# Four residual graph layers on one core: a division of the last projection put under program order, and the denominators of the second half placed at later tiles

## The chip, the core and the metric

The kernel runs on one core of a Trainium2 chip. The core's engines are TensorE (PE, with its weight loads), VectorE (DVE), ScalarE (ACT), GpSimd (POOL) and SyncE (SP, which here only issues DMAs). The metric is the device time of one launch in microseconds. Times of several launches are given by their median; one launch was also taken by the hardware profiler, and all lines of the trace come from that one.

## The reference

A graph of N = 3327 nodes with 512 features a node goes through four layers. Each computes `x = layernorm(x + layer(x, adj))`, row by row.

```
def _L2_gnn_ref(h, adj, W, a):
    ...
    Wh = (h @ W).reshape(n, H, D)
    a1, a2 = (a[0, :, :D], a[0, :, D:])
    s1 = jnp.einsum('nhd,hd->nh', Wh, a1)
    s2 = jnp.einsum('nhd,hd->nh', Wh, a2)
    e = jax.nn.leaky_relu(s1[:, None, :] + s2[None, :, :], negative_slope=ALPHA)
    att_logits = jnp.where(adj[:, :, None] > 0, e, NEG_BIG)
    attention = jax.nn.softmax(att_logits, axis=1)
    h_prime = jnp.einsum('ijh,jhd->ihd', attention, Wh)
    return jax.nn.elu(h_prime.reshape(n, H * D))
...
    x = _layernorm(x + _L0_gnn_ref(x, adj, L0_gnn_W, L0_gnn_a), axis=-1)
    x = _layernorm(x + _L1_gnn_ref(x, adj, L1_gnn_W_nb, L1_gnn_b_nb, L1_gnn_W_line, L1_gnn_b_line, 64), axis=-1)
    x = _layernorm(x + _L2_gnn_ref(x, adj, L2_gnn_W, L2_gnn_a), axis=-1)
    x = _layernorm(x + _L3_gnn_ref(x, adj, L3_gnn_W, L3_gnn_a), axis=-1)
    return x
```

Layers 0, 2 and 3 are such attentions (8 heads of 64, 8 of 64, 4 of 128; layer 0 has no elu). Layer 1 takes the mean over the first 64 neighbours of each node and adds two linear maps with a leaky relu.

The kernel leaves the division by the softmax's sum until after `att @ h`: it collects the unnormalised rows (`hd` in HBM) and the sums, and divides when the rows are read for the next layer. elu is computed as `max(h, 0) + min(exp(h), 1)`, whose constant of one falls out in the layernorm that follows.

## The kernel before

**Tiles.** The rows are cut into NT = 26 tiles of 128, counted from 0, so "the fifth tile" is tile 4. The first 13 (tiles 0 to 12) and the last 13 (tiles 13 to 25) are the two halves; the attention works on one half's output rows at a time.

**Stages in time.** Projection of layer 0 (to about 143 us), attention 0 (to 960), the `sage` stage of layer 1 (linear maps to about 1155, then the sums over neighbours to 1620), attention 2 (from about 1640 to 2552), the last projection in `third` (2552 to 2690), attention 3 and the last norms (to the end). Between two layers a "finish" turns the attention's raw rows into the next layer's input.

**The finish (`finish_steps`, L165 to L203, and `norm_rows`, L146 to L161)** takes a pair of tiles, t0 and t0+1. Its steps are:
- `load`: `h` of both tiles from `hd` (L126, on SP in the last projection), and the residual input `xr` from POOL.
- `divide(s)`: on DVE, `h` times the reciprocal of the sums `rec` (L181). With elu, ACT's `e = exp(h)` follows (L186). If `pinned` is set, `exp` of s = 0 is kept in program order.
- `add(s)`: on DVE, L194 and L195 with elu, L197 without.
- `norm_rows` for both tiles together: statistics of each on DVE (L152, L153), one square root on ACT for the pair (L154), reciprocal and product on DVE (L155, L158), then scale and shift of each tile on ACT (L161). As the square root and the two small DVE steps are shared, neither tile of a pair is ready before both have been divided and added.

Exp and square root are in different tables of ACT; a change between them shows as ACT_TABLE_LOAD.

**The last projection (`third`, L892 to L942).** Its loop goes over pairs t0 = 0, 2, ..., 24. Groups of finish steps are loaded ahead by `load_group` (L911): pairs 2 and 4 before the loop, pair t0+6 in iteration t0. Each tile is stored (L133, SP), transposed on PE (`project1`, L261), copied out of PSUM by ACT (`xT`, L262) and summed by DVE (`xsum`, L263). After the first tile of a pair, the finish of the next waiting pair is put in. Then the tile before is multiplied by the weights (`project2`, L271: sixteen matmuls), ACT takes three small columns (L272, L275), and DVE makes `vt` in two pieces (L277), which SP stores (L283). After tile 14 `prepare` and `cut` (L299 to L352) set up the first half of the attention, with transposes of its columns on PE (L312) and their copies by ACT (L314). `mean` (L286) ends the stage. In `load_group`, `pinned` is set for the pair t0 = 2 alone.

**The second half's sums.** Attention 0 and 2 leave two steps in `late` (L541): `place`, 16 small DMAs that bring the sums of tiles 13 to 25 into SBUF (L517, on SP), and `finish_sums` (L525 to L538), five DVE instructions that make their reciprocals. `sage` (L757) and `third` (L923) take these two steps out of the list at t0 = 4 and t0 = 8. Tile 13, the first that needs them, is the second of the pair t0 = 12.

**What orders the work.** PE's instructions run in program order. Those of the other engines are put in order by a scheduler when the program is built, by its own estimates of when each is ready; `tc.keep_in_program_order(ins)` takes an instruction out of its hands, so that it stays behind what the program wrote before it on that engine.

Of the kernel before, what the change touches and what calls it, by code (L numbers as in the profile page):

```python
# [32 lines left out]
def kernel(  # L33
# [10 lines left out]
    nc = tc.nc  # L44
# [74 lines left out]
    def load_tile(dst, src, t, eng):  # L119

        if src.shape[0] == N and t == NT - 1 and LAST < P:
            nc.gpsimd.memset(dst, 0.0)
            for a, z in _row_pieces(LAST):
                eng.dma_start(out=dst[a:z, :], in_=src[t * P + a:t * P + z, :])
        else:
            eng.dma_start(out=dst, in_=src[t * P:(t + 1) * P, :])  # L126
# [38 lines left out]
    def finish_steps(pool, xin, layer, t0, n, hbufs=6, eng=nc.sync, xbufs=None, xpool=None, ebufs=None, pinned=False):  # L165
        H, D = layer.H, layer.D
        ys, xs, steps = [], [], []

        def load():
            for t in range(t0, t0 + n):  # L170
                h = pool.tile([P, F], F32, name="h", bufs=hbufs)
                load_tile(h, hd, t, eng)
                ys.append(h)
                xr = xpool.tile([P, F], F32, name="xr", tag="hb") if xpool else \
                    pool.tile([P, F], F32, name="xr", bufs=xbufs)
                load_tile(xr, xin, t, nc.gpsimd)
                xs.append(xr)

        def divide(s):
            h = ys[s]  # L180
            nc.vector.tensor_tensor(h.rearrange("p (h d) -> p h d", h=H), h.rearrange("p (h d) -> p h d", h=H),  # L181
                                    rec[:, t0 + s, :H].rearrange("p (h e) -> p h e", e=1).to_broadcast([P, H, D]),
                                    op=ALU.mult)
            if layer.elu:
                e = pool.tile([P, F], F32, name="e", bufs=ebufs)
                ins = nc.scalar.activation(e, h, AF.Exp)  # L186
                if pinned and s == 0:
                    tc.keep_in_program_order(ins)
                xs.append(e)

        def add(s):
            h, xr = ys[s], xs[s]
            if layer.elu:
                nc.vector.scalar_tensor_tensor(xr, xs[n + s], 1.0, xr, op0=ALU.min, op1=ALU.add)  # L194
                nc.vector.scalar_tensor_tensor(h, h, 0.0, xr, op0=ALU.max, op1=ALU.add)  # L195
            else:
                nc.vector.tensor_tensor(h, h, xr, op=ALU.add)  # L197

        steps.append(load)
        for s in range(n):  # L200
            steps += [lambda s=s: divide(s), lambda s=s: add(s)]
        steps.append(lambda: norm_rows(pool, ys, t0))
        return ys, steps  # L203
# [482 lines left out]
    def sage(first, first_pool, xin, prev, nxt, wsrc, dst):  # L686
# [3 lines left out]
        with tc.tile_pool(name="sg_z", bufs=1, reuse_waits="tile") as zp, \  # L690
# [21 lines left out]
            with tc.tile_pool(name="sa_w", bufs=1, reuse_waits="tile") as wp, \  # L712
                    tc.tile_pool(name="sa", bufs=2, reuse_waits="tile") as fp, \
                    tc.tile_pool(name="sa_t", bufs=2, reuse_waits="tile") as sp, \
                    tc.tile_pool(name="sa_ps", bufs=2, space=PSUM, reuse_waits="tile") as ps:
                wn = load_w(wp, wnT, "wn", nc.gpsimd)
                wl = load_w(wp, wlT, "wl", nc.gpsimd)
                blb = wp.tile([P, F], F32, name="blb")
                nc.gpsimd.dma_start(out=blb, in_=bl.to_broadcast([P, F]))

                def step1(xt):
                    pt = ps.tile([P, FC, P], F32, name="pt")
                    for c in range(FC):
                        nc.tensor.transpose(pt[:, c, :], xt[:, c * P:(c + 1) * P], ident)  # L724
                    xT = sp.tile([P, FC, P], F32, name="xT")
                    nc.scalar.copy(xT, pt)  # L726
                    return xT

                def step2(xt, xT, t):
                    pz = ps.tile([P, F], F32, name="pz")  # L730
                    for c in range(FC):
                        nc.tensor.matmul(pz, xT[:, c, :], wn[:, c, :], start=c == 0, stop=c == FC - 1)  # L732
                    pi = ps.tile([P, F], F32, name="pi")
                    for c in range(FC):
                        nc.tensor.matmul(pi, xT[:, c, :], wl[:, c, :], start=c == 0, stop=c == FC - 1)  # L735
                    nc.scalar.copy(zs(t, 0), pz)
                    r1 = sp.tile([P, F], F32, name="r1")
                    nc.vector.tensor_tensor(r1, pz, zs(t, 0), op=ALU.subtract)
                    nc.scalar.copy(zs(t, 1), r1)
                    z3 = sp.tile([P, F], BF, name="z3")  # L740
                    nc.vector.tensor_tensor(z3, r1, zs(t, 1), op=ALU.subtract)
                    nc.sync.dma_start(out=zd[t * P:(t + 1) * P, :], in_=z3)
                    xi = sp.tile([P, F], F32, name="xi")
                    nc.vector.tensor_tensor(xi, pi, blb, op=ALU.add)
                    nc.vector.scalar_tensor_tensor(xi, xi, 0.01, xi, op0=ALU.mult, op1=ALU.max)
                    nc.vector.tensor_tensor(xi, xi, xt, op=ALU.add)
                    nc.sync.dma_start(out=xid[t * P:(t + 1) * P, :], in_=xi)


                cr = fp.tile([NT, P], BF, name="cr", bufs=1)  # L750
                nc.sync.dma_start(out=cr, in_=ctd[NT:NT + 1, :].rearrange("o (t p) -> (o t) p", p=P))
                cnt = zp.tile([P, 3, NT], F32, name="cnt")
                pend = None
                ahead = first
                for t0 in range(0, NT, 2):
                    ys = ahead
                    if t0 in (4, 8):  # L757
                        prev.late.pop(0)(fp)
                    if t0 == 8:
                        cf = fp.tile([NT, P], F32, name="cf", bufs=1)  # L760
                        nc.scalar.copy(cf, cr)
                        pt = ps.tile([P, FC, P], F32, name="pt")
                        cb = pt[:, 0, :NT]
                        nc.tensor.transpose(cb, cf, ident[:NT, :NT])
                        nc.vector.tensor_scalar(cnt[:, 0, :], cb, NEIGHBOURS, 1.0, op0=ALU.min, op1=ALU.max)
                        nc.vector.reciprocal(cnt[:, 1, :], cnt[:, 0, :])
                        nc.vector.tensor_scalar(cnt[:, 2, :], cb, 0.0, None, op0=ALU.is_gt)
                    for s, y in enumerate(ys):
                        xT = step1(y)
                        if s == 0 and t0 + 2 < NT:  # L770
                            ahead = finish(fp, xin, prev, t0 + 2, 2, 6, nc.sync if t0 else nc.gpsimd)
                        if pend:
                            step2(*pend)
                        pend = (y, xT, t0 + s)
                step2(*pend)
            first_pool.close()

            with tc.tile_pool(name="sb_w", bufs=1, reuse_waits="tile") as wp, \
# [69 lines left out]
                for b in range(len(blocks)):  # L848
                    t0, i0 = blocks[b]
# [42 lines left out]
    def third(first):  # L892
        with tc.tile_pool(name="col3", bufs=1) as cp, tc.tile_pool(name="at_r3", bufs=2, reuse_waits="tile") as rp:
# [3 lines left out]
            with tc.tile_pool(name="p_w", bufs=1, reuse_waits="tile") as wp, \  # L897
# [13 lines left out]
                def load_group(t0):  # L911
                    if t0 < NT:
                        groups.append(finish_steps(fp, x2, L2, t0, 2, 10, nc.gpsimd if t0 < 4 else nc.sync, 6,
                                                    pinned=t0 == 2))
                        groups[-1][1].pop(0)()

                load_group(2)
# [2 lines left out]
                load_group(4)  # L920
                for t0 in range(0, NT, 2):
                    ys = ahead
                    if t0 in (4, 8):  # L923
                        L2.late.pop(0)(fp)
                    load_group(t0 + 6)
                    for s, y in enumerate(ys):
                        t = t0 + s
                        store_tile(x3, y, t, nc.sync)
                        xT = L3.project1(pp, ps, y, t)
                        if s == 0 and groups:  # L930
                            ahead, steps = groups.pop(0)
                            for f in steps:
                                f()
                        if pend:
                            L3.project2(pp, bank, wsb, *pend)
                        pend = (xT, t)
                        if t == HALF + 1:
                            L3.prepare(pp, 0)
                            L3.first_rows = L3.rows(rp, 0, 0)
                            L3.cut(pp, 0)  # L940
# [284 lines left out]
```

## Time and profile before

| | us |
|---|---|
| median of 3 launches | 3389.97 |
| lowest, highest | 3388.6, 3393.65 |
| the profiled launch's own time | 3389.15 |
| its span in the trace | 3387.4 |
| PE, DVE, ACT busy in the span | 3251.2, 2687.5, 2354.6 |
| last projection, 2552 to 2690: PE, DVE, ACT busy in 138 us | 119.66, 111.95, 100.71 |
| linear maps of `sage`, 960 to 1155: PE, DVE, ACT busy in 195 us | 179.47, 129.87, 66.36 |

The profile is read like this. The page gives the busy time of each engine and its costliest groups; the waits list says which engine stood idle ahead of which line, and what it waited for; the timeline lists instructions in order of time with the start, the time taken, the engine, the line and the tiles written and read, and in brackets the idle time just before. Several equal instructions in a row are merged into one row with their count. The mean clock that PE was granted over the whole launch was 0.985 of full speed; in the last projection 0.91, in the linear maps of `sage` 0.96.

### The profile page before, as it was taken

The numbers are of one execution on the slowest core, as the hardware profiler recorded it, in microseconds if no ns is written. First come the engines' busy times: TensorE is split into PE (matmuls) and PEld (weight loads), VectorE is DVE, ScalarE is ACT, GpSimd is POOL, SyncE is SP. The second block draws the span as 40 slices with busy tenths as digits, with TensorE's granted clock in tenths as the row PEclk, the third lists the DMA queues.
The fourth block names the chain that finished last, engine by engine and source line by source line (L and its number), as shares of the span: only waits on it lengthen the run. The fifth ranks groups of instructions, "written<-read, shape, count | busy, mean of one in ns | idle before, by whom it ended". The sixth has DMA issues, their size and how long they took to land.

```text
span 3387.4 us, 47182 instructions
## 1 busy us (share of the span) xinstructions
PE 3251.2 (96%) x18476; PEld 1626.4 (48%) x18476; DVE 2687.5 (79%) x2619; ACT 2354.6 (70%) x2143; POOL 239.8 (7%) x389
## 2 busy tenths in 40 slices
PE   8899999999979999999989999999998999999997
PEld 7634344444434445545544444444446754455453
DVE  5799999999967544444449999999998766668887
ACT  2398998999953333333338999999997655558986
POOL 3100000000010011111110000000002000010110
PEclk9999999999999999999999999999998999999998
DMA  9644111110143343333320111111117411122211
GB/s 368 222 124 127 49 49 38 55 49 28 44 123 125 122 117 84 91 85 87 80 77 20 47 48 50 51 48 47 35 31 241 152 41 42 41 51 80 94 42 49
DMA packets 288014, 284.29 MB, mean 84 GB/s; under 512 B 107492, under 2 KB 223534, under 8 KB 287791
## 3 DMA queue, kind: packets, MB, share of 16 engines
q1 hardware_dynamic: 254063, 170.62, 16.6%
q0 software_dynamic: 28208, 102.96, 9.5%
q10 hardware_dynamic: 5520, 7.69, 0.7%
q8 instruction: 146, 2.39, 0.3%
q14 instruction: 77, 0.63, 0.1%
HBM read 212.01 MB, written 69.17 MB: 83 GB/s over the span
## 4 chain that ended last, share of the span: by engine, by line
PE 85%; DVE 5%; DMA 4%; ACT 3%; issue 2%; SPq 0%; ACTq 0%; DVEq 0%; POOL 0%; POOLq 0%
PE po L428 52%; PE acc L859 12%; PE pd L380 7%; PE pw L271 5%; DVE t L405 3%; PE pz L732 3%; DMA raw<-in_adjT_dram 3%; PE pi L735 3%; ACT y L408 1%; PE pt L456 1%; PE pk L819 1%; DMA h<-hd 0%; PE pa L1108 0%; PE pt L724 0%; PE pct L664 0%
## 5 line engine op out<-in xcount | busy, mean ns | idle before, releaser
L405 DVE SCALAR_TENSOR_TENSOR t<-rb,qc,mask 128x1664 f32<-128x1664 f32 x1040 | 1960.3, 1954 | 169.4 <-PE po L428 147.3
L408 ACT ACTIVATE y<-t,bi,sc 128x1664 fp8e4<-128x1664 f32 x1040 | 1769.5, 1766 | 310.4 <-PE pd L380 292.7
L428 PE MATMUL po<-t,vj 128*64 128x448 f32 (+3 forms) x8320 | 1909.6, 521 | 22.1 <-DVE t L405 19.6
L428 PEld LDWEIGHTS po<-t,vj 128*64 128x64 f32 (+1 forms) x8320 | 838.9, 148 | 970.6 <-issue 704.0
L859 PE MATMUL acc<-zs,kt 128*128 128x512 bf16 x1352 | 401.1, 380 | 0.0
L271 PE MATMUL pw<-wsb,xT 128*128 128x264 f32 (+1 forms) x1248 | 302.2, 397 | 15.2 <-DVE vt L277 12.0
L859 PEld LDWEIGHTS <-kt 128*128 128x128 fp8e4 x2002 | 196.1, 98 | 242.1 <-issue 7.7
L811 ACT CAST pk<-cy 128x512 f32<-128x512 bf16 x169 | 99.0, 588 | 277.4 <-DVE kt L823 266.3
L271 PEld LDWEIGHTS pw<-wsb,xT 128*128 128x128 f32 x1248 | 241.1, 197 | 60.7 <-ACT xT L262 10.8
L380 PE MATMUL pd<-y,sden 128*32 128x448 fp8e4 (+1 forms) x4160 | 259.5, 342 | 10.4 <-ACT y L408 10.4
L859 PE MATMUL acc<-zl,kt 128*128 128x512 bf16 x650 | 246.5, 379 | 0.0
L380 PEld LDWEIGHTS <-sden 128*32 128x32 bf16 x4160 | 117.5, 96 | 162.5 <-issue 139.8
L823 DVE SCALAR_TENSOR_TENSOR kt<-pk,mask 128x512 fp8e4<-128x512 f32 x169 | 116.1, 688 | 94.0 <-PE pk L819 94.0
L277 DVE TENSOR_TENSOR vt<-pw,dc 128x256 f32<-128x256 f32 x156 | 59.0, 418 | 148.2 <-ACT dc L272 143.7
L359 POOL DMA_DIRECT2D rb<-r x40 | 21.3, 532 | 1670.4 <-DVE t L405 1652.2
L275 ACT COPY rc<-pw 128x8 f32<-128x8 f32 (+1 forms) x78 | 12.6, 162 | 156.6 <-PE pw L271 154.1
L831 DVE SCALAR_TENSOR_TENSOR y<-acc,cnt,bnb 128x512 f32<-128x512 f32 x26 | 19.5, 751 | 97.7 <-PE acc L859 90.3
L732 PE MATMUL pz<-wn,xT 128*128 128x512 f32 x208 | 94.9, 600 | 1.7 <-ACT xT L726 1.7
L700 POOL DMA_DIRECT2D cy<-ctd x91 | 67.9, 746 | 385.1 <-ACT pk L811 312.6
L735 PE MATMUL pi<-wl,xT 128*128 128x512 f32 x208 | 93.5, 592 | 0.0
L634 DVE TENSOR_SCALAR mask<-raw 128x832 fp8e4<-128x832 int32 (+2 forms) x90 | 54.8, 614 | 38.9 <-DMA raw<-in_adjT_dram 38.5
L154 ACT ACT_TABLE_LOAD x45 | 57.7, 1283 | 37.0 <-DVE mv L153 36.4
(187 smaller groups left out, 1699.3 us busy)
## 6 DMA issues: line engine op xcount, KB each, us to landing
vj<-v SPq DMA_DIRECT2D x312, 128.0 KB
rb<-r POOLq DMA_DIRECT2D x40, 832.0 KB, 4.8
raw<-in_adjT_dram SPq DMA_DIRECT2D x67, 416.0 KB
cy<-ctd POOLq DMA_DIRECT2D x78, 256.0 KB, 4.0
h<-hd SPq DMA_DIRECT2D x61, 256.0 KB
v<-vt SPq DMA_DIRECT2D x50, 256.0 KB
hd<-hb SPq DMA_DIRECT2D x48, 256.0 KB
xr<-x POOLq DMA_DIRECT2D x45, 256.0 KB, 3.1
```

The source lines that it names most:

```text
L271: nc.tensor.matmul(pw[e][:, :FW + H], xT[:, c, :], wsb[:, c, e, :], start=c == 0, stop=c == FC - 1)
L277: nc.vector.tensor_tensor(vt[:, hs, :], pw[e][:, :FW].rearrange("p (h d) -> p h d", d=D), self.dc[:, t, hs].rearrange("p (h e) -> p h e", e=1)
L380: nc.tensor.matmul(pd[c][32 * kk:32 * kk + 32, :w_], lhsT, rhs, start=(kk, c) not in seen, skip_group_check=final is not None, stop=last a ...
L405: nc.vector.scalar_tensor_tensor(t, rb[k], self.qc[:, j, h:h + 1], mask[:, j, i0:i0 + IW], op0=ALU.max, op1=ALU.mult)
L408: nc.scalar.activation(y, t, AF.Sigmoid, bias=self.bi[:, j, h:h + 1], scale=self.sc[:, j, h:h + 1], saturate=False)
L428: nc.tensor.matmul(po[c][k * D:(k + 1) * D, :z - a_], vj[:, j % 2, k * D:(k + 1) * D], ts[k][:, a_:z], start=j == 0, stop=j == NT - 1)
L700: nc.gpsimd.dma_start(out=cy[:, :n, :], in_=ctd[t:t + n, b * GW:(b + 1) * GW] .rearrange("(o t) i -> o t i", o=1).to_broadcast([P, n, GW]))
L732: nc.tensor.matmul(pz, xT[:, c, :], wn[:, c, :], start=c == 0, stop=c == FC - 1)
L735: nc.tensor.matmul(pi, xT[:, c, :], wl[:, c, :], start=c == 0, stop=c == FC - 1)
L811: nc.scalar.copy(pks[k % 2], carry[b, t // 4 * 4][:, t % 4:t % 4 + 2, :])
L823: nc.vector.scalar_tensor_tensor(kt, pk, NEIGHBOURS, mask[:, t:t + 2, i0:i0 + GW], op0=ALU.is_le, op1=ALU.mult, saturate=False)
L859: nc.tensor.matmul(acc, kts[t][:, s * P:(s + 1) * P], zs(t, c) if c < 2 else zl[:, t, :], start=t == 0 and c == 0, stop=t == NT - 1 and c ...
```

## The change

Two things are changed.
- In `finish_steps`, the division of a pair's first tile is kept in program order whenever `pinned` is true, and the exp only when it is 2. In `load_group`, the pair t0 = 2 gets 2 (division and exp pinned), the pair t0 = 4 gets True (division alone), and all others False. The program puts the finish of the pair 4 behind the norm of the pair 2 and behind `xsum` of tile 2.
- The two `late` steps are taken at t0 = 6 and t0 = 10, both in `sage` and in `third`.

```
--- before.py
+++ after.py
@@ -178,13 +178,15 @@
 
         def divide(s):
             h = ys[s]
-            nc.vector.tensor_tensor(h.rearrange("p (h d) -> p h d", h=H), h.rearrange("p (h d) -> p h d", h=H),
+            ins = nc.vector.tensor_tensor(h.rearrange("p (h d) -> p h d", h=H), h.rearrange("p (h d) -> p h d", h=H),
                                     rec[:, t0 + s, :H].rearrange("p (h e) -> p h e", e=1).to_broadcast([P, H, D]),
                                     op=ALU.mult)
+            if pinned and s == 0:
+                tc.keep_in_program_order(ins)
             if layer.elu:
                 e = pool.tile([P, F], F32, name="e", bufs=ebufs)
                 ins = nc.scalar.activation(e, h, AF.Exp)
-                if pinned and s == 0:
+                if pinned == 2 and s == 0:
                     tc.keep_in_program_order(ins)
                 xs.append(e)
 
@@ -754,7 +756,7 @@
                 ahead = first
                 for t0 in range(0, NT, 2):
                     ys = ahead
-                    if t0 in (4, 8):
+                    if t0 in (6, 10):
                         prev.late.pop(0)(fp)
                     if t0 == 8:
                         cf = fp.tile([NT, P], F32, name="cf", bufs=1)
@@ -911,7 +913,7 @@
                 def load_group(t0):
                     if t0 < NT:
                         groups.append(finish_steps(fp, x2, L2, t0, 2, 10, nc.gpsimd if t0 < 4 else nc.sync, 6,
-                                                    pinned=t0 == 2))
+                                                    pinned=(t0 == 2) * 2 or t0 == 4))
                         groups[-1][1].pop(0)()
 
                 load_group(2)
@@ -920,7 +922,7 @@
                 load_group(4)
                 for t0 in range(0, NT, 2):
                     ys = ahead
-                    if t0 in (4, 8):
+                    if t0 in (6, 10):
                         L2.late.pop(0)(fp)
                     load_group(t0 + 6)
                     for s, y in enumerate(ys):
```

More of the change, by code (lines that the diff above doesn't have):

```diff
@@ L180, in divide @@
             h = ys[s]
-            nc.vector.tensor_tensor(h.rearrange("p (h d) -> p h d", h=H), h.rearrange("p (h d) -> p h d", h=H),
+            ins = nc.vector.tensor_tensor(h.rearrange("p (h d) -> p h d", h=H), h.rearrange("p (h d) -> p h d", h=H),
                                     rec[:, t0 + s, :H].rearrange("p (h e) -> p h e", e=1).to_broadcast([P, H, D]),
                                     op=ALU.mult)
+            if pinned and s == 0:
+                tc.keep_in_program_order(ins)
             if layer.elu:
@@ L186, in divide @@
                 ins = nc.scalar.activation(e, h, AF.Exp)
-                if pinned and s == 0:
+                if pinned == 2 and s == 0:
                     tc.keep_in_program_order(ins)
@@ L756, in sage @@
                     ys = ahead
-                    if t0 in (4, 8):
+                    if t0 in (6, 10):
                         prev.late.pop(0)(fp)
@@ L913, in load_group @@
                         groups.append(finish_steps(fp, x2, L2, t0, 2, 10, nc.gpsimd if t0 < 4 else nc.sync, 6,
-                                                    pinned=t0 == 2))
+                                                    pinned=(t0 == 2) * 2 or t0 == 4))
                         groups[-1][1].pop(0)()
@@ L922, in third @@
                     ys = ahead
-                    if t0 in (4, 8):
+                    if t0 in (6, 10):
                         L2.late.pop(0)(fp)
```

## The prediction

> **What bounds the kernel now.** I read the page first (TensorE busy in 96% of the span, and no table of slices shows a hole), then the waits of the last projection, 2552 to 2690 us, then each engine's instructions there in order of time. The projection computes one tile of 128 rows at a time on PE: four transposes (L261), sixteen matmuls of the tile before (L271). [...] First the waits of that window (total us, times, longest):
>
> ```profile
> DVE h L181 <- DMA h<-hd: 6.1, 3, 4.5
> ...
> PE pt L261 <- ACT h L161: 11.8, 2, 8.5
> ```
>
> PE waits for normalised rows, and DVE once for a load. PE in order of time (start, us, in brackets the idle time before):
>
> ```profile
> 2573.51 1.12 PE L261 MATMUL pt<-ident,h 128*128 128x128 f32 x4 [8.46 <-ACT h L161]
> 2574.42 5.42 PE L271 MATMUL pw<-wsb,xT 128*128 128x260 f32 x16
> 2579.68 0.60 PE L261 MATMUL pt<-ident,h 128*128 128x128 f32 x4
> 2580.12 3.67 PE L271 MATMUL pw<-wsb,xT 128*128 128x260 f32 x16
> 2583.63 0.60 PE L261 MATMUL pt<-ident,h 128*128 128x128 f32 x4
> ...
> 2601.26 3.77 PE L271 MATMUL pw<-wsb,xT 128*128 128x260 f32 x16 [0.98 <-ACT xT L262]
> ...
> 2616.71 0.60 PE L261 MATMUL pt<-ident,h 128*128 128x128 f32 x4
> 2618.61 3.75 PE L271 MATMUL pw<-wsb,xT 128*128 128x260 f32 x16 [1.30 <-ACT xT L262]
> ...
> 2634.75 0.75 PE L312 MATMUL pr<-ident,rc 128*4 128x128 f32 x5 [3.64 <-ACT rr L314]
> 2635.34 0.60 PE L261 MATMUL pt<-ident,h 128*128 128x128 f32 x4
> 2635.77 5.36 PE L271 MATMUL pw<-wsb,xT 128*128 128x260 f32 x16
> ```
>
> Tiles 2, 4 and 12 start their transposes at 2573.51, 2583.63 and 2616.71. From transpose to transpose a tile takes 3.95 us (2583.63 less 2579.68); the one after the long wait 6.17. After tile 15 every row follows without a wait, so the stage ends as late as PE's waits make it. Now DVE and ACT:
>
> ```profile
> 2562.96 1.40 DVE L181 TENSOR_TENSOR h<-h,rec 128x512 f32<-128x512 f32 x2 [4.52 <-DMA h<-hd]
> 2564.28 0.69 DVE L194 SCALAR_TENSOR_TENSOR xr<-e,xr 128x512 f32<-128x512 f32 x1
> ...
> 2602.73 0.20 DVE L532 SCALAR_TENSOR_TENSOR rec<-pes,rec 128x52 f32<-128x52 f32 x1
> ```
> ```profile
> 2572.65 1.52 ACT L161 ACTIVATE h<-h,rs 128x512 f32<-128x512 f32 x2
> ...
> 2578.36 1.52 ACT L161 ACTIVATE h<-h,rs 128x512 f32<-128x512 f32 x2 [0.16 <-DVE rs L158]
> ...
> 2615.69 1.52 ACT L161 ACTIVATE h<-h,rs 128x512 f32<-128x512 f32 x2 [0.79 <-DVE rs L158]
> ```
>
> DVE stood 4.52 us on tile 4's division with the additions of tiles 2 and 3 behind it. The three ACT rows end the norms of the pairs (2,3), (4,5), (12,13). The first of two is done after some 0.81 us: tile 4 at 2579.17, 4.5 us before PE takes it; tile 12 at 2616.50, 0.2 us before. One has room, the other none.
>
> [...] sixteen matmuls take 3.67 us, but 5.42 after 8.46 idle and 5.36 after 3.64; 3.75 after 1.30. [...] The trace has 1.28 us[...]. I use 1.28.
>
> **The change part by part.** From the instruction order of both built programs: PE's is identical, POOL swaps one pair. In the last projection DVE, ACT and SP change; in the sage stage the denominators move.
>
> *Tile 2.* The pinned division of tile 4 leaves its place, but the unpinned divisions of tiles 5, 6 and 7 move up into it, ahead of the additions of 2 and 3. Tile 4's load is in at 2562.96; 256 KB follow each other at some 400 GB/s (the page of 2550 to 2572 us shows 385 to 411 there), so 0.65 us apart: estimate 2563.6, 2564.3, 2564.9 for 5, 6, 7. The additions start at 2565.6, 1.3 later than now. Then six steps (L194, L195, L152 twice each) of 0.60 = 3.6, aggregation and one projection piece 0.45: 2569.65. Today's last aggregation is at 2569.60, since today a fourth division and others lie between. The norm's later steps stand behind four divisions and end as today: tile 2 at 2573.5, gain 0. Bounds: 3.0 earlier if the divisions find their loads by 2561, 1.3 later if the 1.3 is passed on. Value 0.
>
> *Tile 4.* Its division now stands behind xsum of tile 2. From PE's 2573.51: transposes 1.07, ACT copy 0.6, xsum 0.65, division 0.69, Exp table 1.28, exp 0.63 are 4.92: 2578.4. Two L194, two L195, two L152 at 0.60: 3.6; aggregation and projection pieces 0.5: 2582.5; square root and its release 0.5: 2583.0. Reciprocal and L158 stand behind xsum and two L194 of the next pair, 2.5: 2585.5; L161 0.81: 2586.35. PE would take tile 4 at 2583.6: a wait of **2.8**. With nothing standing between the norm's steps it is 0.3 or so. [...] cold tile, at most 1.9 more. I take it.
>
> *Loads.* SP no longer issues 16 small loads of sums (three rows, 4.45 + 2.88 + 1.77 = 9.1 us) ahead of the loads of h for tiles 8 to 11. DVE's waits of 1.03 and 0.59 us for h end, and the stop of 0.98 before tile 7's matmuls, with 0.2 around it: **-1.2**. At t0=6 the 9.1 us lie before stores and loads used two tiles later: 0.
>
> *Tile 12.* finish_sums (L532 to L538) moves from behind the projection piece of tile 6 to behind that of tile 8. Tile 13 is the first of the second half, and shares its norm with tile 12. After the change, from PE's start of tile 10: 1.2 to L532; the sums 2.2; division 0.7; ACT, held by copies, gives exp 1.6 later; L194, L195 and two divisions between 2.5; L152, two projection pieces, aggregation 1.3; table and square root 1.1; reciprocal and L158 behind three additions 1.7; L161 0.9: 13.2 us. PE needs 7.9 for two tiles: a wait of **5.3**. Bounds: with no foreign work between, its own rows and their releases are 8.7 (wait 0.8); with today's 13.8 from the sums (2602.73) to the end of L161 (2616.50), and today's lag of 3.0 of L532 behind PE's start of tile 8 (2599.68), it is 16.8 (wait 8.9). The 1.30 us before tile 11's matmuls goes (**-1.3**), as the copy is long done. A wait of 5.3 makes a cold tile: **+1.9**.
>
> *Before tile 15.* The 3.64 us for rr comes from ACT being behind with two table loads and L161. PE later by 6, ACT is less behind: the wait falls by up to 1.9 and the cold tile behind it (1.7) goes, together 0 to -3.6; I take **-1.8**.
>
> *Sage.* Today L532 is at 1032.90, and tile 13's division follows only at 1043.82; from there to L161's first end (1048.9) are 5.1. Two tiles of 7.31 later (1059.04 less 1051.74, PE's rows there) L532 stands at 1047.5; the sums take 2.1, and then 5.1: 1054.7. PE takes tile 12 at 1059.04. Cost 0; cover 4.3. Without that cover each microsecond over costs one.
>
> Sum: 2.8 + 1.9 - 1.2 + 5.3 - 1.3 + 1.9 - 1.8 = **+7.6 us**. PE has no slack after that: the end moves by as much. The profiled execution took 3389.15 us (span 3387.4 and 1.75 around it), 0.8 under the median of 3389.97. So 3396.8 beside it, **3397.6** as a median.
>
> **The rivals.** (A, forecast) Both new waits on PE: 3397.6, 3394 to 3400.
> (B, not slower) Tile 12's chain is short. Place: tile 12's transposes; price 5.3 + 1.9. It decides when the chain of 13.2 comes under 10 (a wait of 2.1[...]), because DVE, done with other tiles' additions early, has little between finish_sums and L161. At 8.7, with tile 4 not cold and rr as now: 2.8 - 1.2 + 0.8 - 1.3 = +1.1: 3391. For it: DVE loses its load waits. Against: today 13.8 us pass there, with room 0.2.
> (C, faster) The freed DVE carries through: the loads are in by 2561, tile 2 gets its norm 3.0 earlier, PE's wait falls to 5.5; with B's short chain, only 0.3 before tile 4 (2.5 less) and the -3.6 in full: -3.0 + 1.1 - 2.5 - 3.6 = -8.0: 3382. For it: the 4.52 wait did stand on the path. Against: divisions 5 to 7 wait for the same train of loads. The pin doing not what it says, other divisions filling the hole, is thus part of A.
> (D, slower still) All of tile 12's 8.9 us, and nothing back at rr: 7.6 + 3.6 + 1.8 = +13.0: 3403.
>
> **How the numbers follow.** A 0.52, B 0.18, C 0.10, D 0.20. This kernel's measurement tells 0.2% (6.8 us: 3383.2, 3396.8) from no change. Of A 0.10 lies below 3396.8, the rest and D are slower; C is faster. Faster 0.10, within 0.28 (B, 0.10 of A), slower 0.62. Range 3389 to 3403: it leaves out C and what of D goes beyond its 13.0.
>
> **What would show it.** A: PE's wait before tile 2 stays near 8.5; a new one of 2 to 3 before tile 4; one of 4 to 7 before tile 12, each on L161; L532 some 11 us later; the waits of 0.98 and 1.30 gone; in the sage stage no new wait. It is wrong if tile 2 starts before 2571, or if PE takes tile 12 without a wait; then B or C holds. If PE waits in sage for L161 at tile 12, the cover of 4.3 was misread.

## The result and the profile after

The changed kernel takes 3394.76 us in the median (3392.5 to 3400.38, 12 runs), the kernel before 3389.03 us (3386.02 to 3393.65, 12 runs, the three of above among them). The ratio is 1.0017, with a 95% interval of 1.0009 to 1.0024: slower by some 5.7 us. The forecast was 7.6 us slower, so the direction held, and the two waits that it rests on came; the size stayed a microsecond under the bound of 0.2% (6.8 us) that was drawn for "slower", so of the three outcomes the one given 0.28 came, not the one given 0.62. The profiled execution has a span of 3392.0 us.

In the changed kernel the line numbers behind L183 are higher by two: L188 is the exp, L196 and L197 are the additions, L263 the transposes, L264 xT, L265 xsum, L273 the matmuls, L316 the copies of the columns' transposes (rr), L534 to L540 the reciprocals of the sums. PE is called cold where it is granted half of its clock, and warm where it is granted all of it: a matmul of the last projection takes 0.64 us cold and 0.38 warm in these traces. The waits of the last projection, 2552 to 2695 us:

```profile
PE pt L263 <- ACT h L161: 17.5, 3, 9.9
...
DVE h L181 <- DMA h<-hd: 3.8, 1, 3.8
```

The list before has two waits of PE for L161, 11.8 us in all, but one of them is 3.4 us ahead of tile 0; after the change that one (3.2 us) is put down to the load of the weights and isn't in the 17.5. Like for like it is one wait of 8.5 us before and three of 17.5 in all now. DVE's long wait for loads is shorter (3.8 instead of 4.5), and alone. PE in order of time shows where the new wait is:

```profile
2574.23 1.11 PE L263 MATMUL pt<-ident,h 128*128 128x128 f32 x4 [9.94 <-ACT h L161]
2575.14 5.67 PE L273 MATMUL pw<-wsb,xT 128*128 128x260 f32 x16
...
2587.22 0.65 PE L263 MATMUL pt<-ident,h 128*128 128x128 f32 x4 [2.46 <-ACT h L161]
2587.71 3.67 PE L273 MATMUL pw<-wsb,xT 128*128 128x260 f32 x16
...
2603.59 3.67 PE L273 MATMUL pw<-wsb,xT 128*128 128x260 f32 x16
...
2624.16 1.11 PE L263 MATMUL pt<-ident,h 128*128 128x128 f32 x4 [5.06 <-ACT h L161]
2625.07 4.61 PE L273 MATMUL pw<-wsb,xT 128*128 128x260 f32 x16
...
2640.55 1.20 PE L314 MATMUL pr<-ident,rc 128*4 128x128 f32 x5 [1.13 <-ACT rr L316]
2641.55 1.06 PE L263 MATMUL pt<-ident,h 128*128 128x128 f32 x4
2642.40 4.48 PE L273 MATMUL pw<-wsb,xT 128*128 128x260 f32 x16
```

Read the brackets: 2.46 before tile 4 and 5.06 before tile 12 are new. The stop of 0.98 before tile 7's matmuls (2603.59) is gone, and so is the one of 1.30 behind tile 12. The wait before tile 2 has become longer, 9.94 for 8.46, although tile 2 is not later: PE's work before it ended 1.8 us earlier, counted from the end of the attention. The row behind 2.46 us takes 3.67, as fast as ever; the row behind 5.06 takes 4.61.

The engines that make these waits, DVE first and then ACT:

```profile
2564.31 1.94 DVE L181 TENSOR_TENSOR h<-h,rec 128x512 f32<-128x512 f32 x3 [3.82 <-DMA h<-hd]
2566.17 1.29 DVE L196 SCALAR_TENSOR_TENSOR xr<-e,xr 128x512 f32<-128x512 f32 x2
...
2576.00 0.69 DVE L265 TENSOR_REDUCE xsum<-xT 128x4 f32<-128x512 f32 x1 [2.67 <-ACT xT L264]
2576.60 0.68 DVE L181 TENSOR_TENSOR h<-h,rec 128x512 f32<-128x512 f32 x1
2579.31 1.29 DVE L196 SCALAR_TENSOR_TENSOR xr<-e,xr 128x512 f32<-128x512 f32 x2 [2.02 <-ACT e L188]
...
2612.18 0.20 DVE L534 SCALAR_TENSOR_TENSOR rec<-pes,rec 128x52 f32<-128x52 f32 x1
```
```profile
2573.36 1.52 ACT L161 ACTIVATE h<-h,rs 128x512 f32<-128x512 f32 x2 [2.55 <-DVE rs L158]
...
2577.35 1.28 ACT L188 ACT_TABLE_LOAD   x1 [1.39 <-DVE h L181]
...
2586.35 1.52 ACT L161 ACTIVATE h<-h,rs 128x512 f32<-128x512 f32 x2 [1.03 <-DVE rs L158]
...
2623.30 1.52 ACT L161 ACTIVATE h<-h,rs 128x512 f32<-128x512 f32 x2 [1.58 <-DVE rs L158]
```

The hole that tile 4's division left is filled by three others (the row of three at 2564.31, whose first waits 3.82 us for its load), and the additions of tiles 2 and 3 still stand behind it. Tile 4's division stands alone at 2576.60, behind xsum of tile 2, and the change of table (1.28 us in the trace of either kernel) waits for it. From PE's start of tile 2 to the end of tile 4's L161 (the first of the two in the row at 2586.35, 0.81 us) are 12.93 us (2587.16 less 2574.23; worked out: 12.84).

On SP, the small loads of the sums (L517, after the change L519) did not move as the program has it. Before:

```profile
2562.35 0.32 SPq L126 DMA_DIRECT2D h<-hd  x1
...
2563.72 0.32 SPq L126 DMA_DIRECT2D h<-hd  x1
2566.00 4.45 SPq L517 DMA_DIRECT2D pes<-dd  x7
```

and after:

```profile
2563.60 2.32 SPq L126 DMA_DIRECT2D h<-hd  x4
2566.71 3.15 SPq L519 DMA_DIRECT2D pes<-dd  x5
...
2601.27 0.55 SPq L519 DMA_DIRECT2D pes<-dd  x1
```

In `place` the first of the 16 DMAs alone is kept in program order. One DMA moved, from 2587.54 to 2601.27; the other 15 are issued where they were, between 2566 and 2579. What changed ahead of them is that, behind the first four that both kernels have, four more loads of `h` come first instead of two.

To set the two kernels side by side, count from the last group of transposes that ends the attention (L456 before, at 2551.68; L458 after, at 2552.71). The start of the mean's matmuls ends the stage (2684.38 and 2690.13). The projection takes 132.70 us before and 137.42 after, **4.7** more. In steps, each the shift of PE's transposes against the tile before: up to tile 2 -0.3; tile 3 +0.2; tile 4 +2.6; to tile 8 -0.1; tile 9 -1.25; tile 12 +5.2; tile 13 -0.1; tile 15 -1.1; tile 16 -0.5; from there 0. The other 1.0 of the 5.7 is within the interval of the ratio. The spans of the two profiled executions differ by 4.6 us.

The sage stage, DVE, ACT and PE of the changed kernel:

```profile
1046.78 0.21 DVE L534 SCALAR_TENSOR_TENSOR rec<-pes,rec 128x52 f32<-128x52 f32 x1
```
```profile
1053.12 1.52 ACT L161 ACTIVATE h<-h,rs 128x512 f32<-128x512 f32 x2
```
```profile
1059.13 0.60 PE L726 MATMUL pt<-ident,h 128*128 128x128 f32 x4
```

The sums have moved by 13.9 us (from 1032.90), tile 12 is ready at 1053.9, and PE takes it at 1059.13 without a wait.

### The profile page after: what moved, and what is told of

It reads as the page before. It is cut to its first block, busy times and chain, and to the rows that moved or that the text cites. A ratio compares the mean times of both kernels' runs of the same rounds, so it can differ in the third digit from the quotient of the medians.

```text
span 3392.0 us, 47134 instructions
## 1 busy us (share of the span) xinstructions
PE 3248.9 (96%) x18424; PEld 1629.3 (48%) x18476; DVE 2688.2 (79%) x2619; ACT 2357.9 (70%) x2145; POOL 239.7 (7%) x389
## 4 chain that ended last, share of the span: by engine, by line
PE 83%; DVE 5%; issue 4%; DMA 4%; ACT 3%; POOL 0%; SPq 0%; ACTq 0%; POOLq 0%; DVEq 0%
PE po L430 50%; PE acc L861 12%; PE pd L382 7%; PE pw L273 6%; DVE t L407 3%; PE pz L734 3%; PE pi L737 3%; DMA raw<-in_adjT_dram 2%; ACT y L410 1%; PE pk L821 1%; PE pt L458 1%; PE pt L263 0%; PE pa L1110 0%; PE pt L726 0%; DMA dd<-red 0%
## 5 line engine op out<-in xcount | busy, mean ns | idle before, releaser
L861 PE MATMUL acc<-zs,kt 128*128 128x512 bf16 x1312 | 392.9, 381 | 2.0
L273 PE MATMUL pw<-wsb,xT 128*128 128x264 f32 (+1 forms) x1248 | 300.2, 396 | 12.9 <-DVE vt L279 12.1
L273 PEld LDWEIGHTS pw<-wsb,xT 128*128 128x128 f32 x1248 | 240.6, 196 | 56.8 <-issue 9.8
## 6 DMA issues: line engine op xcount, KB each, us to landing
vj<-v SPq DMA_DIRECT2D x312, 128.0 KB
```

Source lines behind the costliest of these rows:

```text
L273: nc.tensor.matmul(pw[e][:, :FW + H], xT[:, c, :], wsb[:, c, e, :], start=c == 0, stop=c == FC - 1)
L861: nc.tensor.matmul(acc, kts[t][:, s * P:(s + 1) * P], zs(t, c) if c < 2 else zl[:, t, :], start=t == 0 and c == 0, stop=t == NT - 1 and c ...
```

## The experiments

All were timed in five rounds beside the kernel before. A ratio's interval here is some 0.08% to either side, 2 to 3 us, so most readings rest on PE's rows in one profiled execution each. How far these repeat can be told from kernels with the same program up to a point: up to tile 14, before and "before, prepare later" lie within 0.6 us of each other, and changed and "changed, prepare later" within 0.2; the whole projection of before and of "late in sage alone" differs by 0.2. In all thirteen kernels the median moved the same way as the projection, with sizes at most 3.4 us apart. "First" counts the projection from its first transposes, as the expectations do, and "whole" from the attention's last transposes, which is fairer where the first tiles themselves shift. Waits are those of PE ahead of a tile's transposes; "rr" is the sum of its two stops ahead of the groups of L312.

| kernel | first | whole | tile 2 | tile 4 | tile 10 | tile 12 | rr | ratio to before |
|---|---|---|---|---|---|---|---|---|
| before | 128.5 | 132.7 | 8.46 | 0 | 0 | 0 | 3.64 | 1 |
| changed | 133.4 | 137.4 | 9.94 | 2.46 | 0 | 5.06 | 1.94 | 1.0017 (1.0009 to 1.0024) |
| pin alone | 127.0 | 131.0 | 8.93 | 1.96 | 1.55 | 0.68 | 1.39 | 0.9999 (0.9990 to 1.0007) |
| late alone | 129.9 | 134.0 | 9.97 | 0 | 0 | 3.82 | 2.33 | 1.0005 (0.9997 to 1.0014) |
| late in sage alone | 128.7 | 132.9 | 9.79 | 0 | 0 | 0 | 3.58 | 1.0002 (0.9994 to 1.0010) |
| reciprocals alone late | 130.5 | 134.7 | 9.61 | 0 | 0 | 3.77 | 2.31 | 1.0000 (0.9992 to 1.0009) |
| changed, reciprocals at 8 | 130.7 | 134.8 | 8.61 | 2.80 | 0 | 2.46 | 0.23 | 1.0011 (1.0003 to 1.0020) |
| before, prepare later | 126.3 | 130.5 | 8.68 | 0 | 0 | 0 | 1.00 | 0.9996 (0.9988 to 1.0004) |
| changed, prepare later | 131.2 | 135.2 | 9.95 | 2.46 | 0 | 5.05 | 1.52 | 1.0017 (1.0009 to 1.0024) |
| all divisions ahead | 134.9 | 140.7 | 1.74 | 1.54 | 3.61 | 0 | 6.85 | 1.0032 (1.0020 to 1.0043) |
| additions first | 122.2 | 128.0 | 7.60 | 1.14 | 1.10 | 1.16 | 1.73 | 0.9995 (0.9987 to 1.0003) |
| additions first, prepare later | 125.3 | 131.1 | 7.65 | 1.17 | 1.10 | 1.16 | 0.23 | 0.9999 (0.9990 to 1.0007) |
| that, reciprocals at 6 | 123.8 | 129.6 | 7.39 | 1.05 | 1.10 | 0.72 | 1.36 | 0.9998 (0.9990 to 1.0006) |
| additions first, third pair too | 122.1 | 127.9 | 1.62 | 2.37 | 3.52 | 2.00 | 0.25 | 0.9988 (0.9980 to 0.9997) |

**The pinning alone.** The changed kernel with both late steps back at 4 and 8.

```
-                    if t0 in (6, 10):
+                    if t0 in (4, 8):
```

> The pinning alone; the two late steps stay at t0 = 4 and 8 in both stages. Theory (two separate new waits of PE): before tile 4's transposes PE waits 2.0 to 3.0 us as in the changed kernel; before tile 12's it waits under 0.5, because the sums are made at their old place and PE comes later than before. Against the kernel before: +2.5 for tile 4, less the stops of 1.0 to 1.3 that vanish once PE is later, so +0 to +3 us. Rival (the pin is the whole loss): +5 to +6 us. Rival (the late sums are the whole loss, the pin costs nothing): 0 or faster, and no wait before tile 4.

The wait before tile 4 is there, 1.96 us, and the one before tile 12 nearly gone (0.68); a wait of 1.55 before tile 10, which was not expected, is new. But the stage is 1.7 us shorter than before, not longer. PE's rows at the place of the stop for rr show where the time comes back:

```profile
2633.30 0.75 PE L314 MATMUL pr<-ident,rc 128*4 128x128 f32 x5 [1.22 <-ACT rr L316]
...
2634.33 3.67 PE L273 MATMUL pw<-wsb,xT 128*128 128x260 f32 x16
```

Before, PE stopped 3.64 us there, and the tile behind was cold (5.36); here it stops 0.17 and 1.22, and the tile is warm (3.67): 2.1 and 1.7 us come back by PE's starts of tiles 15 and 16. That it is because PE comes later and ACT is less behind is the likely reason, not one tried by itself here. So the pin by itself makes a wait, and by the median (0.9999) no loss that shows. The first rival falls; of the second, "0 or faster" came true, and "no wait before tile 4" did not.

**The late steps alone.** The kernel before with the steps at 6 and 10.

```
-                    if t0 in (4, 8):
+                    if t0 in (6, 10):
```

> The late steps alone, at t0 = 6 and 10 in both stages; the pinning as before. Theory: no wait before tile 4; DVE's wait of 4.5 for a load of h ahead of tile 2 is there again; before tile 12 PE waits 4 to 6 us for L161, with a partly cold tile behind it. Against the kernel before: about +5 less 1.2 for the loads, less 1.3 and the gain of about 1 at the copies of rr: +2 to +5 us. Rival (pin is the whole loss): 0 within 1 us.

No wait before tile 4; before tile 12:

```profile
2620.44 1.11 PE L261 MATMUL pt<-ident,h 128*128 128x128 f32 x4 [3.82 <-ACT h L161]
2621.35 4.87 PE L271 MATMUL pw<-wsb,xT 128*128 128x260 f32 x16
```

3.82 us, a little under the 4 to 6 expected, and the stage is longer by 1.3, less than the 2 to 5; by the median it is not told apart. DVE's wait for a load of `h` is there as expected, 4.4 us.

From tile 2 to tile 12 the totals of the two parts add up: 43.20 us before, 47.21 with the pin (+4.0), 45.83 with the late steps (+2.6), 49.93 with both (+6.7). That is luck, since the steps inside do not: either part alone takes away the stop at tile 7 (-1.2 at tile 9), and it can go only once; the pin alone has +1.7 at tile 10, and both together nothing there; tile 12 gets +0.8 and +4.0 from the parts and +5.2 from both. Behind tile 12 not even the totals add up: 67.67 before, 63.33 with the pin (-4.3), 66.57 with the late steps (-1.1), 65.97 with both (-1.7). So the late steps cost twice when they come on top of the pin: the wait before tile 12, and what the pin would have got back behind it, since PE is cold at tile 12 then (4.61 for the sixteen matmuls), and again behind rr (4.48).

**The late steps in the sage stage alone.** The same edit at `prev.late` only.

> The late steps moved to t0 = 6 and 10 in the sage stage alone; the last projection is as before. Theory: the norm of tiles 12 and 13 has some 4 us of cover, so no new wait of PE on L161 in 1030 to 1155 us, and the time is that of the kernel before within 1 us. Rival (part of the loss comes from sage): +2 us or more, with a wait before tile 12 or 14 there.

PE waits nowhere in 990 to 1155 us, and the projection takes 132.9. The median is 1.0 us above that of before, at the edge of what was expected and not told apart from 0. But from tile 3 of that stage to its last, PE's transposes take 161.05 us in all fourteen kernels, wherever the late steps stand: sage has no part in the loss.

**The reciprocals alone late.** The last projection's steps at 4 and 10.

```
-                    if t0 in (4, 8):
+                    if t0 in (4, 10):
```

> In the last projection alone: the small loads of sums stay at t0 = 4, the reciprocals of the sums go to t0 = 10; pinning and sage as before. Theory: the same wait of 4 to 6 us before tile 12 as with both late steps moved, and the stop of about 1 us at tile 7 still there, since the small loads still stand ahead of the loads of h: +3 to +6 us against the kernel before, 0 to 1.5 more than with both moved. Rival (the small loads on SP matter, the reciprocals do not): within 1 us of the kernel before and no wait before tile 12.

The wait before tile 12 is the same as with both late (3.77 and 3.82), and the stop at tile 7 is there (0.83). So without the pin the later reciprocals make the whole wait, and the later `place`, by the loads of `h` that then go ahead, takes the stop away. The sum came out lower than expected, +1.95 by the stage and nothing in the median.

**The changed kernel with the reciprocals back at t0 = 8.** The small loads stay at 6.

```
-                    if t0 in (6, 10):
+                    if t0 in (6, 8):
```

> The changed kernel with the reciprocals of the sums back at t0 = 8 in the last projection; the small loads stay at t0 = 6. Theory: the wait of 5.1 us before tile 12 and the cold tile behind it go (under 1.5 left), the wait of 2.5 before tile 4 stays, and since PE is then later by a few us, the stop for rr shrinks as with the pinning alone: the projection takes 126 to 129 us instead of the changed kernel's 133.4. Rival (the small loads, not the reciprocals, make the wait before tile 12): 131 us or more.

Neither was met: 130.7, and a wait of 2.46 us before tile 12. Half of the wait went with the reciprocals. The rest is probably in DVE's order. Here, behind the reciprocals:

```profile
2609.81 0.69 DVE L181 TENSOR_TENSOR h<-h,rec 128x512 f32<-128x512 f32 x1
...
2610.50 0.67 DVE L181 TENSOR_TENSOR h<-h,rec 128x512 f32<-128x512 f32 x1
...
2611.16 2.49 DVE L181 TENSOR_TENSOR h<-h,rec 128x512 f32<-128x512 f32 x4
```

and with the pin alone:

```profile
2604.70 0.66 DVE L196 SCALAR_TENSOR_TENSOR xr<-e,xr 128x512 f32<-128x512 f32 x1
...
2606.61 0.68 DVE L181 TENSOR_TENSOR h<-h,rec 128x512 f32<-128x512 f32 x1
```

Six divisions follow the reciprocals in one kernel, with only two short steps of a norm between; in the other an addition and the norm before come first. In the last projection the two programs differ in the place of the small loads alone, and the scheduler answers with another order on DVE. With the pin, then, moving the small loads is enough to make a wait before tile 12 (0.68 to 2.46). How much of the 2.46 the six divisions make was not tried, nor were the small loads moved without the pin.

**The preparation later.** Both original kernels with the first half's columns prepared two tiles later.

```
-                        if t == HALF + 1:
+                        if t == HALF + 3:
```

> The kernel before with the preparation of the first half's columns two tiles later (after tile 16 instead of 14); all else as before. Theory (the stop of 3.6 us for rr and the cold tile behind it come from ACT being behind at that place, and are a reserve that any earlier delay of PE eats): two tiles later ACT and DVE are less behind, the stop falls below 2 us and the tile behind is not cold: 123 to 126 us for the projection instead of 128.5. Rival (the stop belongs to the preparation itself wherever it stands): 3 us or more again, 128 to 129.

> The changed kernel with the preparation of the first half's columns two tiles later. Theory (the reserve at rr is mostly eaten already in the changed kernel: 1.9 us of stop and 0.8 of cold matmuls left): 0.5 to 2.5 us less than the changed kernel, 131 to 133 us for the projection, so that the difference between this pair of kernels is 6 to 9 us, more than the 4.9 between the original pair. Rival (nothing is shared between the waits): the difference stays at 5.

The stop fell, from 3.64 to 1.00 us and from 1.94 to 1.52, the tile behind it is warm in both, and both kernels became shorter by 2.2 us by the stage (not told apart in the median). The difference between them stayed, 4.7 by the stage, so the theory of one reserve that earlier delays eat is not borne out there; the medians, 7.1 us apart, lie in the 6 to 9 of the theory, but with some 3 us of noise on each they can't decide it. What a kernel gets back behind tile 12 depends on the order there, and I have no rule for it.

**All divisions ahead.** A pair's divisions put in one pair earlier, behind the norm of the pair before and ahead of the first transposes of that pair, all pinned. Exp is no longer pinned and has four buffers, here and in the four kernels below; what these two do by themselves was not tried. The lines that move the divisions:

```
+                        if s == 0 and groups:
+                            steps = groups[0][1]
+                            steps.pop(0)()
+                            steps.insert(0, steps.pop(1))
+                            steps.pop(0)()
```

> From the kernel before: the divisions of every pair are put one pair ahead, all pinned behind the norm of the pair before and ahead of the first transposes of that pair's tiles, with four buffers for exp; late steps at t0 = 4 and 8 as before. Theory: with no division of tiles 4 to 9 ahead of the additions of tiles 2 and 3, PE's wait before tile 2 falls from 8.5 to 3.5 to 5.5 us, and there is no wait before tile 4, because its divisions no longer stand behind xsum of tile 2: the projection, from its first transposes to the matmuls of the mean, takes 124 to 127 us instead of 128.5. Rival (the loads of h set when tile 2 is ready, whatever the order): the wait before tile 2 stays at 8 us or more.

The first half came true: 1.74 us before tile 2. The rest did not; the stage is 8 us longer. Its waits:

```profile
PE pt L261 <- ACT h L161: 19.1, 9, 5.0
...
DVE xr L194 <- ACT e L188: 15.8, 10, 1.8
```

Divisions, exps, additions and norm of a pair now follow each other without other work between, and DVE waits ten times for an exp (L188 in this kernel). PE stops 1.4 to 1.7 us ahead of the pairs at tiles 2 to 8, then 3.61 at tile 10, 1 to 2 us at tiles 14, 22 and 24, and 4.92 ahead of the first group of L312. It seems that the scheduler's own order, with divisions put ahead, covered these.

**The additions first.** The same for tiles 4 to 7 alone; the rest left to the scheduler. Against the kernel just shown:

```
-                        if s == 0 and groups:
-                            steps = groups[0][1]
+                        if t == 0:
+                            for _, steps in groups[:2]:
```

> From the kernel before: the divisions of tiles 4 to 7 alone (not those of all pairs) pinned behind the norm of tiles 2 and 3 and ahead of tile 2's transposes, with four buffers for exp; the other pairs are left to the scheduler, late steps at t0 = 4 and 8. Theory (putting all divisions ahead lost by making each pair's norm a chain of its own, 1.4 us of wait per pair, while the first pair gained 9): PE's wait before tile 2 is 2 to 6 us instead of 8.5, and the later pairs run at 3.95 us a tile as before, with stops at tile 12 and at rr: 122 to 127 us for the projection instead of 128.5, 2 to 6 us off the median. Rival (what is gained at tile 2 comes back as waits at the next pairs, since the same loads and norms are waited for there): 128 us or more.

122.2 us as expected, but not by the wait named: that is still 7.60. The median is 2.7 us under that of before, not told apart. DVE tells why the wait stayed:

```profile
2566.27 0.18 DVE L153 BATCH_NORM_AGGREGATE mv<-st 128x2 f32<-128x6 f32 x1
2572.41 1.35 DVE L181 TENSOR_TENSOR h<-h,rec 128x512 f32<-128x512 f32 x2 [5.96 <-DMA h<-hd]
2573.68 0.16 DVE L155 RECIPROCAL rs<-rs 128x2 f32<-128x2 f32 x1
```

The additions are done by 2566.3, but now the divisions of tiles 8 and 9 were put ahead of the reciprocal, and wait for two loads that SP issues only at 2566.79. By PE's rows, from the attention's last transposes to tile 2 it is 1.9 us less than before, from there to tile 12 1.8 more, and from tile 12 to the end of the stage 4.6 less, as with the pin alone.

**With the preparation later, and with the reciprocals earlier.** Both on top of that.

> The same with the preparation of the first half's columns two tiles later (after tile 16). Theory: another 2 us less, as the move alone gave (126.3 instead of 128.5): 120 to 125 us. Rival (ACT, behind by more once PE comes earlier, stops PE at another place): no gain over the kernel with the additions first.

> As that one, and the reciprocals of the sums at t0 = 6 instead of 8 (small loads at t0 = 4). Theory (the later the reciprocals, the longer the wait before tile 12; earlier ones leave none): no wait before tile 12, and 0 to 3 us less than with the sums at t0 = 8. Rival (DVE, waiting for the small loads at the earlier place, holds up the norms behind it): a wait for the load of the sums in DVE of over 1 us and no gain.

The rival of the first holds: 3.1 us are lost by the stage, with a new wait of 2.77 before tile 16. The earlier reciprocals bring 1.5 of it back, with 0.72 instead of 1.16 before tile 12; "no wait" was expected there.

**The third pair too.** The additions first, and the divisions of tiles 8 and 9 pinned behind the norm of tiles 4 and 5. Against the additions first:

```
-                            for _, steps in groups[:2]:
+                            for _, steps in groups[t // 2:2]:
```

> As the kernel with the additions first, and the divisions of tiles 8 and 9 as well are pinned, behind the norm of tiles 4 and 5. In the kernel with the additions first DVE had the statistics of tiles 2 and 3 at 2566.4, and then stood 5.96 us on the division of tile 8 for its load, with the reciprocal of the norm behind it. Theory (what makes tile 2 late is only what the scheduler puts ahead of its norm, not the norm): PE's wait before tile 2 falls from 7.6 to 1 to 3 us, the tile behind is warm, and 3 to 7 us of it stay: 116 to 120 us for the projection from its first transposes, against 122.2 for the kernel with the additions first and 128.5 for the kernel before; 5 to 11 us less than before in the median. Rival (the time comes back as waits at the next pairs): 121 us or more, with waits of over 2 us at tiles 4, 8, 10 or 12.

```profile
2568.14 0.66 PE L261 MATMUL pt<-ident,h 128*128 128x128 f32 x4 [1.62 <-ACT h L161]
...
2578.63 0.66 PE L261 MATMUL pt<-ident,h 128*128 128x128 f32 x4 [2.37 <-ACT h L161]
...
2607.05 0.66 PE L261 MATMUL pt<-ident,h 128*128 128x128 f32 x4 [3.52 <-ACT h L161]
...
2618.84 0.66 PE L261 MATMUL pt<-ident,h 128*128 128x128 f32 x4 [2.00 <-ACT h L161]
```

The wait before tile 2 is down to 1.62 us. The rows show what the rival said: 2.37 before tile 4, 3.52 before tile 10, 2.00 before tile 12, and the stage ends where it did with two pairs: up to tile 2 it gains 7.8 us on the kernel before, up to tile 12 it gives 7.5 of them back, and the 4.5 that stay are again those behind tile 12. In the median it is 3386.53 us beside 3390.61: 4.1 us less, under the 5 to 11 expected. It is the one kernel here whose interval lies below 1, and only just (0.9997), out of twelve that were tried, so the gain is likely rather than shown.

## Why the prediction was right, and where its sum was off

- **Tile 2, gain 0:** right. The other divisions filled the hole, the first of them waited for its load, and tile 2 came 0.3 earlier. Two kernels with the additions first (all divisions ahead, and the third pair too) have tile 2 some 7.8 us earlier, so this order, not the norm, held it. The waits line has three waits of DVE for loads, not one; the two short ones, 1.03 and 0.59, are named under "Loads".
- **Tile 4, a wait of 2.8:** 2.46, by the chain as worked out. With the pin alone 1.96, with the late steps alone none: shown.
- **Tile 4 cold, +1.9:** this term was mis-sized. The row behind the wait takes 3.67 us, so it costs 0. That is 1.9 of the 2.9 us by which the stage (4.7) stays under the forecast. That a wait of 2.8 us leaves PE cold was an estimate: the kernel before has 3.75 us for the sixteen matmuls behind a stop of 1.30 and 5.36 behind one of 3.64, and no stop near 2.8.
- **Loads, -1.2:** -1.25 at tile 9, but not in the way that was forecast. SP still issues 15 of the 16 small loads between 2566 and 2579; two more loads of `h` go ahead of them. The pin alone loses the same stop (-1.24 at tile 9) with the small loads at their old place, as PE is 1.5 us later there.
- **Tile 12, a wait of 5.3:** 5.06, with 13.06 us from PE's start of tile 10 to the end of L161 (2624.11 less 2611.05) for the 13.2 worked out. Without the pin the reciprocals alone make such a wait (3.77): shown. The small loads by themselves were not tried; on top of the pin they make 2.46 instead of 0.68.
- **The stop at tile 11, -1.3, and tile 12 cold, +1.9:** together -0.1 at tile 13, as the cold tile cost 1.4. This is 0.7 of the 2.9.
- **Before tile 15, -1.8:** -1.6, in two steps. The pin alone gets 3.8 back there, which fits the argument (PE later, ACT less behind); the size is not to be had from the two kernels' sums.
- **Sage, 0 with 4.3 us of cover:** 5.2 of cover, and no wait.

Of the rivals, B and C asked for a short chain at tile 12; it was as long as worked out. D's longest chain (8.9) did not come. What I did not foresee is that the parts don't add up: the pin alone makes its wait and yet is no loss that shows. The two waits carry the sum. The smaller terms are off by 2.9 us together, and that the median (5.7) lies nearer to the forecast than PE's rows (4.7) is luck.

## What to carry to other kernels

A pin on one instruction left a hole that the scheduler filled with the next of the same kind; to free what stood behind, all that it might put there had to be held. A step placed later in the program moves only as far as the scheduler lets it: of 16 DMAs, one moved. Such a step has to be compared with the room of the first tile that needs it, through every tile that shares its norm: here that room was 0.2 us in one stage and 10 in another, for the same edit. And when a stage has a stop further on that a delay shortens, a wait's cost is only known at the stage's end.

## What the runs showed of the hardware

How long a wait must be to leave PE cold could not be told from its length alone. After 2.46 us before tile 4 of the changed kernel the sixteen matmuls took 3.67 us; after the same 2.46 before tile 12, with the reciprocals back at 8, they took 5.04:

```profile
2624.28 1.02 PE L263 MATMUL pt<-ident,h 128*128 128x128 f32 x4 [2.46 <-ACT h L161]
2625.09 5.04 PE L273 MATMUL pw<-wsb,xT 128*128 128x260 f32 x16
```

After longer waits the same sixteen took 4.61 (5.06 us), 4.87 (3.82) and 6.17 (3.77). The clock that PE was granted goes with these times. In the changed kernel it was 1.00 from 2587.22 to 2591.38 us, from tile 4's transposes to the end of the matmuls behind them (3.67), 0.74 in the mean from 2624.16 to 2629.52 at tile 12 (4.61), and 0.72 from 2640.55 to 2646.72 behind the stop for rr (4.48). With the reciprocals back at 8 it was 0.50 from 2624.43 to 2627.84, within the row of 5.04. What sets when the clock falls behind such a wait was not shown. After the waits of 2.46 to 5.06 us named here the sixteen matmuls took from 0 to 2.5 us more than 3.67, and the longest wait did not cost the most.
